# Two graph layers on one core: the neighbours' rows of three tiles in eight are fetched from DRAM by index instead of being selected by one-hot matmuls

## The chip, the cores and the metric

The kernel runs on one core of one Trainium2 chip. The metric is the device time of one execution in microseconds (us); lower is better. Three executions of the kernel before the change took 2499.42, 2499.82 and 2503.61 us, so the median is 2499.82 us.

Names of engines in this document: PE is TensorE (matmuls and transposes; PEld is its weight load), DVE is VectorE, ACT is ScalarE, POOL is GpSimd, SP is the engine that issues the DMAs of the kernel before. "L499" is line 499 of the kernel.

## The reference, cut to what matters

There are 16 graphs ("images" below) of 1024 nodes with 64 features each, and a 1024x1024 matrix of small integers for each graph that tells which nodes are neighbours. Two attention layers follow each other, each with a residual and a normalisation of the rows.

```python
x = -0.0005207 + 1.001 * jax.random.normal(..., (16, 1024, 64), jnp.float32)
_a = jax.random.bernoulli(..., 0.00390625, (16, 1024, 1024))
_a = jnp.logical_or(_a, jnp.swapaxes(_a, -1, -2))
adj = jnp.logical_or(_a, jnp.eye(1024, dtype=bool)).astype(jnp.int32)

def _L0_gnn_ref(atom_embeddings, edges, Wq, bq, Wk, bk, Wv, bv, edge_bias, Wp, bp):
    q = (atom_embeddings @ Wq + bq).reshape(b, m, h, d)      # h = 8 heads, d = 64
    k = (atom_embeddings @ Wk + bk).reshape(b, m, h, d)
    v = (atom_embeddings @ Wv + bv).reshape(b, m, h, d)
    scores = jnp.einsum('bmhd,bnhd->bhmn', q, k) * scale
    scores = scores + jnp.transpose(edge_bias[edges], (0, 3, 1, 2))
    scores = jax.nn.leaky_relu(scores, NEG_SLOPE)
    scores = jnp.where((edges > 0)[:, None, :, :], scores, -1000000000.0)
    attn = jax.nn.softmax(scores, axis=-1)
    out = jnp.einsum('bhmn,bnhd->bmhd', attn, v).reshape(b, m, h * d)
    return out @ Wp + bp

def _L1_gnn_ref(h, adj, lin_w, lin_b, W_w, a):
    hp = jnp.einsum('bni,oi->bno', h, lin_w) + lin_b
    s = u[:, :, None, :] + v[:, None, :, :]                  # u, v: hp times the halves of W_w
    e = jnp.einsum('bijf,f->bij', jnp.where(s > 0, s, ALPHA * s), a[:, 0])
    attention = jax.nn.softmax(jnp.where(adj > 0, e, NEG_INF), axis=2)
    return jax.nn.elu(jnp.einsum('bij,bjf->bif', attention, hp))

x = _layernorm(x + _L0_gnn_ref(x, adj, ...))
x = _layernorm(x + _L1_gnn_ref(x, adj, ...))
```

The matrix has few entries: a node has about eight neighbours among 1024, and itself.

## The kernel before

**Groups and slots.** The kernel does not compute all 1024x1024 scores. It puts the 1024 nodes of an image into 128 groups of 8 consecutive nodes (GR = 8). For each group it lists the columns that any of its 8 nodes needs, in 120 *slots* (SLOTS): 112 for neighbours, which are found from the matrix, and 8 for the group's own nodes. Scores, exponentials and weighted sums are taken over these 120 slots. A mask (`finish`, L423) blanks the slots that belong to another node of the group.

**Tiles and steps.** The 128 groups of an image make 8 *tiles* (t = 0 to 7) of 16 groups: two halves n of the partitions, 8 groups q in each. One loop, L883, runs over g = 8b + t, b being the image. In one step layer 0 works on several tiles at different stages (gather of tile g, turn and score of tile g - 1, exponentials and weights of tile g - 2, output of tile g - 3), and layer 1 does the same for the image before, 12 steps later (LAG). The order of the instructions of every engine is the order in which the loop writes them; no scheduler changes it. Each engine works through its own list in order, so an instruction that waits holds all behind it on the same engine.

**Lists.** `prepare(b)` (L308) builds the lists of an image: DVE turns the matrix into keys and takes the largest of them eight at a time. It is a generator; `Lists.place` (L858) is called at five places of each step and advances it by so many pieces that image b's 41 pieces (PIECES, dealt out by QUOTA) are done two steps before its first tile. After a piece that yields "sums" it goes on only at the step's last place, because the next piece needs a PSUM bank that PE's weighted sums use. The result, `col`, goes to DRAM (`col_d`, L397), one row of column numbers for each group.

**The gather that is changed.** For a tile, SP loads its lists broadcast to all 128 partitions (`load`, L460: 544 KB, tile `cb`); DVE compares them twice with the partition number, which gives the one-hot matrix `f` (`indicate`, L468, L475); PE multiplies the image's rows, split into three bf16 parts (`t3`), with it (`gather`, L488, L499: 26 matmuls for each half of the slots), and ACT copies the result to `xg` (L505), which has features on the partitions and slots in the rows. `own` (L481, L484) has POOL copy the group's own 8 nodes into the last slots. A step later `turn` (L509, L518, L519) transposes `xg` on PE into `xn`, with slots on the partitions, in 8 transposes and two copies on ACT. `score` reads `xg`, `attend` reads `xn`. Layer 0 and layer 1 each do all this for every tile, with buffers of their own.

**What else POOL does, in its order in a step.** The divisions of tile g - 2 (`divide`, L637), one for each half, each waiting for DVE's reciprocal; when lists are built, the blanking of the diagonal (L327); in step t = 2 the normalisation of layer 0's result of the image before (`end`, L697, by L549 to L552), and in steps 6 and 7 layer 1's residual (L820) and normalisation; the own copies of layers 0 and 1 (L484); the row product of layer 1 (`own_rows`, L728); and at the end of steps 2 and 6 the three-part split of the next layer's input (`thirds`, L445, L451 and L453). `place` number 0 is at the start of a step, ahead of the divisions; number 1 after the second division; 2 and 3 before the own copies; 4 after the row product, at the end of the step.

## Time and profile before

One execution was profiled. It took 2508.74 us; its span from the first to the last instruction is 2506.8 us.

| | us | share of the span |
|---|---|---|
| median of three executions | 2499.82 | |
| the profiled execution | 2508.74 | |
| its span | 2506.8 | |
| line 499, the one-hot matmuls on PE | 804.5 | 32% |
| line 475, the equality tests on DVE | 491.6 | 20% |
| line 637, the divisions on POOL | 285.8 | 11% |
| line 518, the transposes of `turn` on PE | 273.9 | 11% |
| line 519, their copies on ACT | 277.3 | 11% |
| line 505, the gather's copies on ACT | 271.5 | 11% |
| line 728, the row products on POOL | 145.9 | 6% |
| line 484, the own copies on POOL | 107.2 | 4% |

The lines count both layers: 256 tiles, of which 128 are layer 0's. Busy time is the time in which an engine has an instruction running; matmuls overlap, so 52 matmuls of 0.28 us each take about 3 us together. PE's granted clock is 0.988 of full speed on average. All DMAs are issued by SP, and together they keep the 16 DMA engines busy for 28.3% of the span; 230.66 MB are moved.

### The profile page before, as it was taken

How to read it: one execution, taken by the hardware profiler on the slowest of the kernel's cores; microseconds unless marked ns; L12 is line 12 of the kernel's file. 1: busy time of each engine (PE TensorE's matmuls, PEld its weight loads, DVE VectorE, ACT ScalarE, POOL GpSimd, SP SyncE). 2: the span in 40 equal slices, each digit the busy share in tenths (PEclk: the TensorE clock that was granted, in tenths of full speed). 3: DMA queues.
4: the chain of work that ended last, by engine and by line, in shares of the span. 5: the costliest groups of instructions: out<-in, count | busy, mean ns of one | idle time of the engine just before them, and what ended most of it. 6: DMA issues, size and time to landing. Idle time of an engine off the chain costs nothing. (4 is left out here: it accounts for less than half of the span.)

```text
span 2506.8 us, 110853 instructions
## 1 busy us (share of the span) xinstructions
PE 2308.1 (92%) x48706; PEld 1957.7 (78%) x48706; DVE 2012.1 (80%) x5237; ACT 1445.2 (58%) x4401; POOL 912.9 (36%) x1106
## 2 busy tenths in 40 slices
PE   5387999999999999999999999999999999999986
PEld 3376788878788887878788787888878888888864
DVE  6687879888888988888898888889888888876642
ACT  0154656656565665656566566656656665666743
POOL 1133333434334343433434343342434434243331
PEclk9998999999999999999999999999999999999998
DMA  3412332423233242323324232332423233221210
GB/s 102 122 59 89 104 103 78 133 77 116 73 102 108 78 133 80 114 73 107 103 78 133 84 109 75 106 103 78 133 86 108 81 100 106 62 92 57 66 52 18
DMA packets 190543, 230.66 MB, mean 92 GB/s; under 512 B 91492, under 2 KB 157092, under 8 KB 190052
## 3 DMA queue, kind: packets, MB, share of 16 engines
q1 hardware_dynamic: 190052, 223.49, 28.3%
q8 instruction: 384, 6.29, 1.0%
q14 instruction: 107, 0.88, 0.1%
HBM read 218.23 MB, written 5.21 MB: 89 GB/s over the span
## 5 line engine op out<-in xcount | busy, mean ns | idle before, releaser
L499 PE MATMUL pg<-f,x 128*64 128x272 bf16 (+2 forms) x13312 | 804.5, 272 | 37.4 <-DVE f L475 34.5
L499 PEld LDWEIGHTS <-x 128*64 128x64 bf16 x13312 | 662.0, 109 | 115.5 <-issue 70.4
L637 POOL TENSOR_TENSOR ls<-ls,den 128x480 f32<-128x480 f32 x256 | 285.8, 1117 | 921.1 <-DVE den L636 912.6
L475 DVE TENSOR_SCALAR f<-cb,jrow 128x2176 bf16<-128x2176 bf16 x512 | 491.6, 1001 | 0.3 <-DMA cb<-col_d 0.3
L505 ACT COPY xg<-pg 128x448 f32<-128x448 f32 x512 | 271.5, 530 | 356.1 <-PE pg L499 355.1
L629 ACT ACTIVATE ls<-ls,mx 128x120 f32<-128x120 f32 x1024 | 391.2, 386 | 4.8 <-DVE mx L620 4.8
L519 ACT COPY xn<-pt 120x512 f32<-120x512 f32 x512 | 277.3, 597 | 11.8 <-PE pt L518 7.1
L751 ACT ACTIVATE r<-pz 128x480 f32<-128x480 f32 x256 | 132.1, 568 | 247.0 <-PE pz L746 247.0
L518 PE MATMUL pt<-ident,xg 128*120 128x128 f32 x2048 | 273.9, 276 | 0.0
L484 POOL COPY xg<-xT 128x64 f32<-128x64 f32 x256 | 107.2, 426 | 387.9 <-PE pt L518 345.4
L518 PEld LDWEIGHTS pt<-ident,xg 128*120 128x120 f32 x2048 | 224.0, 137 | 27.3 <-issue 24.8
L752 DVE SCALAR_TENSOR_TENSOR r<-pz,r 128x480 f32<-128x480 f32 x256 | 155.4, 649 | 50.6 <-ACT r L751 50.6
L629 ACT ACTIVATION_READ_ACCUMULATOR ls<-ls,mx 128x1 f32 x1024 | 194.8, 190 | 0.0
L619 DVE SCALAR_TENSOR_TENSOR ls<-sc 128x480 f32<-128x480 f32 x256 | 191.5, 748 | 0.0
L620 DVE TENSOR_REDUCE mx<-ls 128x4 f32<-128x480 f32 x256 | 167.2, 653 | 8.8
L611 DVE TENSOR_TENSOR sc<-s,rowc 128x480 f32<-128x480 f32 x256 | 155.1, 647 | 22.7 <-PE s L603 21.0
L746 PEld LDWEIGHTS pz<-rw,ub 64*64 64x64 f32 x4096 | 122.6, 133 | 63.9 <-issue 58.5
L655 PE MATMUL z<-w,xn 120*64 120x64 f32 x4096 | 159.2, 227 | 4.4 <-ACT w L647 4.4
L587 DVE TENSOR_TENSOR qp<-pq,qb 128x512 f32<-128x512 f32 x128 | 87.9, 686 | 90.0 <-PE pq L586 89.8
L655 PEld LDWEIGHTS z<-w,xn 120*64 120x64 f32 x4096 | 138.4, 139 | 27.7 <-ACT w L647 19.4
L645 PE MATMUL pp<-ident,ls 128*120 128x128 f32 x1024 | 142.0, 280 | 19.3 <-POOL ls L637 16.6
L740 PE MATMUL pz<-xg,w2d 64*64 64x480 f32 x1024 | 140.4, 588 | 17.1 <-DVE sc L611 17.1
(212 smaller groups left out, 3881.1 us busy)
## 6 DMA issues: line engine op xcount, KB each, us to landing
cb<-col_d SPq DMA_DIRECT2D x256, 544.0 KB
ad<-in_adj_dram SPq DMA_DIRECT2D x256, 256.0 KB
xs<-in_x_dram SPq DMA_DIRECT2D x32, 128.0 KB
rows_s<-slot_d SPq DMA_DIRECT2D x256, 14.0 KB
out_dram<-o SPq DMA_DIRECT2D x32, 128.0 KB
col_d<-col SPq DMA_DIRECT2D x128, 4.2 KB
dg<-in_adj_dram SPq DMA_DIRECT2D x32, 2.0 KB
slot_d<-slot SPq DMA_DIRECT2D x16, 28.0 KB
```

The source lines that it names most:

```text
L475: nc.vector.tensor_scalar(fj.rearrange("p s n q k -> p (s n q k)"), cb.rearrange("p s n q k -> p (s n q k)"), jrow[:, j : j + 1], None, AL ...
L499: nc.tensor.matmul(pg[sub(n), :, FIRST * a_ + lo : FIRST * a_ + to], self.t3[:, k, 4 * hs + 2 * a_ + j, :], f[j][:, 2 * hs + a_, n, :, lo:to],
L505: nc.scalar.copy(dst, pg)
L518: nc.tensor.transpose(pt[:, q, :], xg[:, 4 * m + q, :], ident)
L519: nc.scalar.copy(self.xn[t][:, ts(m, 4), :], pt)
L611: nc.vector.tensor_tensor(sc, both[n], self.rowc[:, n, ts_].unsqueeze(2).to_broadcast([P, 4, SLOTS]), ALU.add)
L619: nc.vector.scalar_tensor_tensor(ls, scs[n], SLOPE, scs[n], ALU.mult, ALU.max)
L620: nc.vector.tensor_reduce(self.mx[:, n, ts_], ls, XX, ALU.max, negate=True)
L629: nc.scalar.activation(ls[:, q, :], ls[:, q, :], AF.Exp, bias=neg[:, q : q + 1], accum_out=den[:, q : q + 1])
L637: nc.gpsimd.tensor_tensor(ls, ls, den.unsqueeze(2).to_broadcast([P, 4, SLOTS]), ALU.mult)
L655: nc.tensor.matmul(zz[sub(n), q, :], xn[:, q, sub(n)], w_[n][:, q // 2, sub(q % 2)], start=True, stop=True)
L752: nc.vector.scalar_tensor_tensor(r, pz[n], SLOPE / (1.0 - SLOPE), r, ALU.mult, ALU.add)
```

## The change

In each image, the tiles T = 2, 5 and 7 of layer 0 no longer get their slots' rows by one-hot matmuls. The five other tiles, and all of layer 1, are unchanged.

A copy of the image's rows is put into a DRAM table with one more row at its front (`table`), in a new place of `start`. `prepare` makes, at its end, a row number for each of the 120 slots of each of the 128 groups, turns it by one PE transpose so that slots lie on the partitions, and keeps it as integers (`at_d`). For a fetched tile POOL issues 16 indirect DMAs, one for each group: each takes 120 row numbers from one column of `at_d` and brings 120 rows of 64 values (256 bytes each) into the group's part of the buffer `xf`, which takes the place of `xn`. The gather of such a tile is then 8 transposes from `xf` into `xg`, and `load`, `indicate`, `own` and `turn` do nothing for it.

```diff
+    FETCHED = {2: (0, 1), 5: (2, 3, 4), 7: (5, 6)}
...
         def place(self, g, k):
+            b, t = divmod(g, NT)
+            for T, steps in FETCHED.items():
+                if b in l0 and t in steps:
+                    i, parts = steps.index(t) * PLACES + k, len(steps) * PLACES
+                    for j in range(2 * NQ * i // parts, 2 * NQ * (i + 1) // parts):
+                        l0[b].fetch(T, j)
             b, t = divmod(g + AHEAD, NT)
...
+        def fetch(self, t, k):
+            if k == 0:
+                self.xn[t] = dbl.tile([SLOTS, NQ, P], F32, tag="xf", bufs=2, name=f"xf_{self.b}_{t}")
+            n, q = divmod(k, NQ)
+            g = D * n + NQ * t + q
+            nc.gpsimd.indirect_dma_start(
+                out=self.xn[t][:, q, sub(n)], out_offset=None, in_=self.table[:, :],
+                in_offset=bass.IndirectOffsetOnAxis(ap=self.at[:, g : g + 1], axis=0),
+            )
...
+        def gather(self, t, hs):
+            if t not in FETCHED:
+                return super().gather(t, hs)
+            nm = f"{self.b}_{t}"
+            if hs == 0:
+                self.xg[t] = dbl.tile([P, NQ, SLOTS], F32, tag="xg0", bufs=2, name=f"xgf_{nm}")
+            pt = ps_g.tile([P, 4, SLOTS], F32, tag="g", name=f"ptf_{nm}_{hs}")
+            for q in range(4):
+                nc.tensor.transpose(pt[:, q, :], self.xn[t][:, 4 * hs + q, :], ident[0:SLOTS, 0:SLOTS])
+            nc.scalar.copy(self.xg[t][:, ts(hs, 4), :], pt)
```

So tile 2 is fetched in steps 0 and 1, tile 5 in steps 2, 3 and 4, tile 7 in steps 5 and 6. The 16 fetches are spread over the places: with two steps, places 0 to 4 of a step issue 1, 2, 1, 2 and 2 fetches; with three, one at each place, and two at the very last. Each half gather needs four groups q of both halves n of the partitions; the last fetches are those that the second half gather needs.

```diff
     def start(b):
...
+        table = dram.tile([N + 1, D], F32, tag="table", bufs=3, name=f"table_{b}")
+        nc.sync.dma_start(table[0:1, :], x[b, 0:1, :])
...
+            nc.sync.dma_start(
+                table[1 : N + 1, :].rearrange("(t n r) d -> n t r d", n=2, r=D)[n],
+                x[b, n * 512 : n * 512 + 512, :].rearrange("(t r) d -> t r d", r=D),
+            )
...
     def prepare(b):
...
+        yield
+        tb = per.tile([P, NSEG, WIN], F32, tag="tb", name=f"tb_{b}")
+        nc.vector.tensor_tensor(tb, seg_at.unsqueeze(2).to_broadcast([P, NSEG, WIN]), win, ALU.subtract)
+        nc.vector.scalar_tensor_tensor(tb, who, 0.5, tb, ALU.is_ge, ALU.mult)
...
+        nc.vector.tensor_copy(av[:, :, 0:FIRST], tv[:, :, 0, 0:FIRST])
+        nc.vector.tensor_tensor(av[:, :, FIRST:WIN], tv[:, :, 0, FIRST:WIN], tv[:, :, 1, 0:SHARE], ALU.max)
+        nc.vector.tensor_copy(av[:, :, WIN:CAP2], tv[:, :, 1, SHARE:WIN])
+        nc.vector.tensor_copy(at_s[:, 2 * CAP2 : SLOTS], own_at)
+        yield "sums"
+        pi = ps_z.tile([SLOTS, P], F32, tag="z", name=f"pi_{b}")
+        nc.tensor.transpose(pi, at_s, ident)
+        at_d = dbl.tile([SLOTS, P], I32, tag="at_d", name=f"at_d_{b}")
+        nc.vector.tensor_scalar(at_d, pi, 0.0, float(N), ALU.max, ALU.min)
```

A few constants for the row numbers (`own_at`, `seg_at`) are made once at the start. Image lists now have 43 pieces instead of 41, and QUOTA gives the two more to its last two steps. Four buffers become fewer: `mask` has 3 instead of 4, and layer 1's `xT`, layer 0's `y` and layer 1's `u` have 1 instead of 2.

## The prediction, made before the changed kernel ran

> **What bounds the kernel now.** I read the engine totals first, then one image's eight steps (b = 7), then that image's event lists. The steps run from one score product of layer 0 (line 603) to the next; in all images but the first they repeat within a few tenths of a us, so one stands for sixteen.
>
> ```profile
> PE 2308.1 (92%) x48706; PEld 1957.7 (78%) x48706; DVE 2012.1 (80%) x5237; ACT 1445.2 (58%) x4401; POOL 912.9 (36%) x1106
> ```
> ```profile
> core 0: us, PE busy (x) PEld busy (x) DVE busy (x) ACT busy (x) POOL busy (x), PEclk, DMA share, GB/s
> 1202.90:1221.33 18.43, 17.82 (x378) 14.99 (x378) 15.13 (x42) 9.55 (x27) 4.58 (x5) 1.00 0.21 68
> 1221.33:1238.72 17.39, 17.39 (x347) 14.39 (x345) 12.22 (x26) 12.58 (x43) 6.32 (x9) 1.00 0.55 185
> 1238.72:1259.16 20.44, 18.75 (x410) 16.03 (x409) 17.97 (x51) 9.77 (x28) 10.38 (x12) 1.00 0.09 31
> 1259.16:1278.26 19.10, 17.25 (x373) 14.96 (x370) 18.64 (x45) 11.83 (x38) 6.05 (x8) 1.00 0.22 68
> 1278.26:1296.70 18.44, 17.44 (x382) 14.88 (x378) 15.91 (x43) 10.62 (x32) 3.77 (x5) 1.00 0.40 127
> 1296.70:1312.26 15.56, 15.56 (x342) 13.69 (x338) 13.27 (x32) 10.87 (x33) 3.84 (x5) 1.00 0.12 41
> 1312.26:1330.18 17.92, 17.92 (x413) 15.63 (x409) 14.54 (x36) 12.02 (x37) 5.30 (x6) 1.00 0.26 69
> 1330.18:1349.36 19.18, 18.66 (x413) 15.50 (x409) 17.25 (x44) 12.95 (x43) 16.60 (x20) 1.00 0.61 202
> ```
>
> The columns are stretch, length, then busy time per engine. In steps 1, 5 and 6 (second, sixth, seventh row) PE is busy for the whole step: a us taken from PE there is a us of the total. In steps 2 and 3 DVE has 17.97 of 20.44 and 18.64 of 19.10, and PE waits on it, so PE time saved there buys less. POOL looks idle, but it holds 16.60 of 19.18 in step 7.
>
> **What is removed.** One fetched tile drops 52 one-hot matmuls (line 499; the 52 of step 5 took 2.98 us) and, a step later, 8 transposes (line 518, 1.04); its new gather does 8 transposes of a similar shape in the old place, 0.55 per half. PE gains 2.98 - 1.10 + 1.04 = 2.9 us a tile. DVE drops two equality tests (line 475, 2 x 1.0) in the step before; ACT trades four copies (2 x 0.53 + 2 x 0.60) for two of 128x480 (about 0.56 each, between those rows); POOL drops one own copy (0.43), SP one load of 544 KB. With all of it on the path, 48 tiles x 2.9 = 140 us.
>
> **What is added and cheap.** Per image: seven DVE operations of at most 128x136, priced by lines 393, 401 and 782 at about 2 x 0.30 + 4 x 0.17 + 0.29 = 1.6 us, in steps 4 and 5, where DVE has over 2 us spare, and against 6 us of tests removed: nothing. One PE transpose, 0.27 (line 780): 16 x 0.27 = 4 us, on the path; it could also wait for DVE's list, but lists are issued places earlier. Three SP issues copying x, 3 x 0.63 (line 290), ahead of the next image's four mask loads; SP spends 340 us waiting for free buffers of those loads, which hides them; without that cover 1.9 us an image. The head, where lists and copies run alone, grows by the 1.6 of DVE and about 3 of SP and landing: 5 us. Buffers cut to one: y waits for a POOL result two steps old, u and xT1 for POOL copies of the same step; before, xT1's copy on ACT ran at 1259.27, 3.5 us after the POOL copy it now waits for, and three fetches stand ahead of that copy. It can be a few tenths late, then delays the exponentials queued on ACT behind it, and ACT is 58% busy. The mask's third buffer is free again a batch earlier: nothing.
>
> **What is added and dear: 48 fetches an image on POOL.** No indirect DMA is in the trace, so two prices are bounded. *c*, POOL's time for one: from below the DMA issues on SP, at 0.57 for the 64-row list (line 397); from above POOL's slowest operation, the power at 1.86 (line 550). Neither is near, so I take the middle, 1.2. *L*, from end of issue to data usable:
>
> ```profile
> 1316.60 0.76 SPq L408 DMA_DIRECT2D slot_d<-slot  x1
> 1320.34 6.14 SPq L415 DMA_DIRECT2D rows_s<-slot_d  x16
> ```
>
> The second is held by the first: 1320.34 - 1317.36 = 3.0 us (mean of 16 waits 48.9/16 = 3.06). At the start, with idle queues, the same pair took 1.16, and the last small row load 1.73 until DVE could use it. L is 1.16 to 3.06; beside running loads the middle of the last two, 2.4.
>
> POOL must issue the last two fetches of a tile after the row product (line 728) of the step before, and PE needs them for its second half gather early in the next step:
>
> ```profile
> 1295.06 1.04 POOL L728 TENSOR_TENSOR ub<-u,in_q 128x512 f32<-128x512 f32 x1
> 1297.89 2.98 PE L499 MATMUL pg<-f,x 128*64 128x272 bf16 x52
> 1300.70 0.28 PE L280 MATMUL back<-lin,aT 128*64 128x64 f32 x4
> ```
> ```profile
> 1321.21 0.99 POOL L637 TENSOR_TENSOR ls<-ls,den 128x480 f32<-128x480 f32 x1 [4.88 <-DVE den L636]
> 1327.18 1.37 POOL L327 TENSOR_TENSOR ab<-ab,no_diag 128x128 bf16<-128x128 bf16 x2 [4.92 <-DVE ab L324]
> 1328.51 1.76 POOL L820 TENSOR_TENSOR y<-y,x 128x512 f32<-128x512 f32 x1
> 1330.21 1.11 POOL L484 COPY xg<-xT 128x64 f32<-128x64 f32 x2
> 1331.29 1.22 POOL L728 TENSOR_TENSOR ub<-u,in_q 128x512 f32<-128x512 f32 x1
> 1332.45 0.60 POOL L451 CAST x<-xs 128x512 bf16<-128x512 f32 x1
> ```
>
> Tile 5 (step 5): row product over at 1296.1, two fetches 2.4, landing 2.4, half gather 0.55: 1301.45. Before, the gather was over at 1300.87. Loss 0.6, less the 1.04 saved in step 6: gain 0.45 us.
>
> Tile 7 (step 7): after the division at 1322.2 come five fetches (6.0), to 1328.2; then what is queued behind them: diagonal mask 1.37, addition 1.76, one own copy 0.5, row product 1.2, to 1333.0; then the last two 2.4, landing 2.4, half gather 0.55: 1338.35 against 1335.07 before (1332.43 + 2.64). Loss 3.3, less 1.04: 2.25. The divisions of step 7 slip too, but PE asks for them later, at some 1342.
>
> Tile 2 (step 2): POOL has slack in steps 0 and 1; counted the same way from the division that ends at 1213.6, the last fetch ends at 1240.8 and lands at 1243.2. PE's second half began at 1244.1, held by DVE's sums (a 1.02 wait of line 671). No stall, but the first half's 0.94 only lengthens that wait; what stays is about 1.0 of the rest, since steps 2 and 3 are DVE's.
>
> Sum per image: 1.0 + 0.45 - 2.25 = -0.8, so +13 us in all; transpose and head +9. DVE is slowed too: a pair of tests beside an idle POOL took 1.47, beside POOL's work 2.24 to 2.74. Steps 2 and 3, DVE's own, hold about six tests each with others; with POOL busy half again as long I take 0.2 more for each of six on the path: 1.2 x 16 = +19. Bounds: none, or 0.5 for each, +48. Altogether 13 + 9 + 19 = +41 on the profiled execution's 2508.74 (span 2506.8): 2550. Its time stands 0.36% above the median, so 2541 there.
>
> The Trainium skill (SBUF — State Buffer, section "SBUF: two separate sides") speaks against the change: while DVE runs a two-port operation, POOL cannot write descriptors, and a DMA of some 620 ns took about 3100. Should that strike both last fetches of tiles 5 and 7 by 2.5 us each, the estimate by that page would be 10 us an image more, some 2700. DMA: Bandwidth & Descriptors (section on the anatomy of one DMA, the gpsimd path) gives about 2.0 us for a whole small DMA; in place of my 3.6 for issue and landing, that estimate would be 3.2 us an image less, about 2490. No run so far shows either.
>
> **Rivals.** *Fetches are short and land early* (c = 0.57, L = 1.16, no DVE slowing): tile 5 has no stall and gains 2.9; tile 7's last pair follows the unchanged 1332.5, is usable at 1335.35 after the half gather, -0.3 + 1.04 = 0.8; tile 2 gives 1.0. 4.7 x 16 = 75 less, 9 back: 2443, or 2434 by the median. With c = 1.0 and L = 1.73: 1.0 + 1.5 - 0.6 = 1.9 an image, 31 less, 9 back, so 2478 by the median. For it: POOL is 36% busy. Against: the place of the last pair, which no small c moves before 1332.5. It ends faster while c stays below about 1.1 and DVE is not slowed. *POOL becomes the bound*: POOL has 57 us of work in an image of 146, and 48c fit while c < 1.85; but steps 0, 1, 5 and 6 take eight each. At c = 1.5, L = 2.5 the same counts give tile 2 -0.5, tile 5 -0.3, tile 7 -4.5: 5.3 x 16 = 85, with 9: 2594 by the median; at 1.86 and 3.06 the sum is about -16 an image, 2764. *The gain and the stalls cancel*: c near 1.15 and no DVE slowing, 2500. That the change does not do what it says is excluded: the issue order shows 48 fetches an image on POOL, and the one-hot products gone.
>
> **How the numbers follow.** Moderate stalls with DVE slowed, the forecast, 2510 to 2570: 0.35. POOL bound, above 2570: 0.20. Short fetches: 0.36. Cancelling: 0.09. A measurement of this kernel tells about 0.2% from no change, so: faster 0.36, same 0.09, slower 0.55. The likeliest case alone spans 2510 to 2570; the range reaches to c of about 0.6 on one side and 1.7 on the other: 2430 to 2640.
>
> **What would show it.** Each second-half transpose of a fetched tile has PE idle before it, waiting for a DMA: 2 to 6 us in step 7, 1 to 3 in step 5, none in step 2. POOL's fetch group has a mean near 1.2 us and POOL's busy time rises from 913 to some 1,800 (913 - 20 + 768 x 1.2). Line 475's mean goes above 1.0 us. Wrong if PE's waits for fetches sum under 30 us, or if POOL is idle when PE waits.

## The result, and the profile after

Four executions of the changed kernel took 2646.8 to 2661.52 us, median 2658.88, beside 2501.72 us for the kernel before: a ratio of 1.0616, 95% interval 1.0579 to 1.0653. It is slower by 6.2%. The forecast was 2541 us; the measured time lies above the top of its range, 2640. The profiled execution's span is 2657.7 us against 2506.8.

The page of the changed kernel: engine totals, the DMA queue of the new fetches, the group of the fetches, and the equality tests.

```profile
PE 2273.4 (86%) x46226; PEld 1890.6 (71%) x46226; DVE 1950.1 (73%) x5261; ACT 1395.9 (53%) x4305; POOL 1681.1 (63%) x1829
...
q0 software_dynamic: 24576, 23.67, 4.9%
...
L611 POOL DMA_INDIRECT xf<-table,at_d x768 | 826.5, 1076 | 202.4 <-issue 187.3
...
L514 DVE TENSOR_SCALAR f<-cb,jrow 128x2176 bf16<-128x2176 bf16 x416 | 360.2, 907 | 0.3 <-DMA cb<-col_d 0.3
```

The priced parts of the fetch came out as forecast: 1.08 us for one, and with the gap before it (202.4/768 = 0.26) 1.34 us; POOL went from 913 to 1681 us. The equality tests (line 475 before, 514 now) did not get slower: 907 ns against 1001. PE lost only 35 us of busy time, where 140 had been counted: part of what is left runs slower, because PE's clock falls, as shown below.

The image b = 7 by steps, with the columns of the table of before; steps 2, 7 and 0 of the next image:

```profile
1161.34:1181.64 20.30, 16.95 (x367) 14.22 (x366) 18.41 (x57) 9.96 (x28) 14.15 (x13) 1.00 0.15 44
...
1254.74:1279.37 24.63, 19.29 (x369) 14.97 (x366) 15.07 (x41) 12.89 (x43) 20.04 (x25) 0.86 0.50 158
1279.37:1296.88 17.51, 16.47 (x370) 14.03 (x369) 15.07 (x43) 8.48 (x25) 9.25 (x10) 1.00 0.18 41
```

Step 7 stands out: PE is busy for 19.29 of 24.63 us, at a granted clock of 0.86, and POOL for 20.04. Over images 2 to 13 the median lengths of the steps, before and after, are:

| step | 1 | 2 | 3 | 4 | 5 | 6 | 7 | 0 |
|---|---|---|---|---|---|---|---|---|
| before, us | 17.66 | 20.40 | 19.09 | 18.44 | 15.56 | 17.93 | 18.77 | 17.58 |
| after, us | 18.31 | 20.88 | 17.80 | 20.09 | 17.06 | 17.45 | 25.11 | 17.52 |

Step 7 alone is 6.34 us longer; the other seven add 2.5 us together. The granted clock changed with them: in these twelve images it fell to half of full speed not once before, and 33 times after, for 157 us together: 12 times in step 7, and 21 times in steps 2 to 5. Step 4, for instance, takes 20.9 us in the six images in which it falls there, and 18.6 to 19.3 in the six others. What PE waited for in the changed kernel (total us, times, longest):

```profile
PE ptf L636 <- DMA xf<-table,at_d: 121.0, 73, 3.9
PE e L845 <- DVE r L831: 50.1, 65, 2.1
PE po L750 <- DVE sc L690: 46.5, 29, 2.1
PE pi L456 <- DVE at_s L453: 38.5, 15, 23.4
```

The first is the new wait for fetched rows. The second and third were 17.7 and 27.7 us before: where PE has less to do, it comes to DVE's results earlier and waits there. The fourth is the new transpose of the row numbers, 23.4 us of it at the head.

PE's instructions at the start of step 7 (start, duration, idle time before and its releaser in brackets). Line 682 is the score product, 636 the new transposes of the gather, 665 and 819 the first two products behind it:

```profile
1254.74 1.05 PE L682 MATMUL s<-xg,qp 64*64 64x120 f32 x32
...
1255.93 0.73 PE L636 MATMUL ptf<-ident,xf 120*128 120x120 f32 x5
1259.49 0.32 PE L636 MATMUL ptf<-ident,xf 120*128 120x120 f32 x1 [2.83 <-DMA xf<-table,at_d]
1262.32 0.72 PE L636 MATMUL ptf<-ident,xf 120*128 120x120 f32 x2 [2.51 <-DMA xf<-table,at_d]
...
1263.24 1.92 PE L665 MATMUL pq<-xT,aqk 128*64 128x64 f32 x32
1265.09 1.88 PE L819 MATMUL pz<-xg,w2d 64*64 64x480 f32 x8
```

Two waits, 5.34 us together, and behind them two groups that took 1.10 and 1.03 us in the steps of before take 1.92 and 1.88. Line 665 starts 8.5 us after the score product here (8.5 to 9.8 in images 1 to 13), against 4.12 in most images before: 4.8 us later at a mean of 8.9. With 0.82 and 0.85 for the two groups that makes 6.5, which is about the whole growth of the step.

POOL's list at the same time, from the third-last fetch of tile 7 on:

```profile
1252.82 1.96 POOL L611 DMA_INDIRECT xf<-table,at_d  x1 [0.30 <-issue]
1254.79 0.82 POOL L349 TENSOR_TENSOR ab<-ab,no_diag 128x128 bf16<-128x128 bf16 x2
1255.57 1.27 POOL L899 TENSOR_TENSOR y<-y,x 128x512 f32<-128x512 f32 x1
...
1256.98 1.03 POOL L807 TENSOR_TENSOR ub<-u,in_q 128x512 f32<-128x512 f32 x1
1258.20 1.03 POOL L611 DMA_INDIRECT xf<-table,at_d  x1 [0.19 <-issue]
1259.53 1.35 POOL L611 DMA_INDIRECT xf<-table,at_d  x1 [0.30 <-issue]
```

The third-last fetch is over at 1254.78, used at 1259.49, so 4.7 us to land, while SP issued four mask loads and two list loads between 1251 and 1256.5. The last two follow the row product (807). The second-last is over at 1259.23 and used at 1262.32, 3.1 us later; the last is over at 1260.88 and landed some 1.7 us later, in time for the last transpose. PE's clock over these microseconds (the number after POOL's count), then the DMA share, which falls as the loads end:

```profile
1259.00:1260.00 1.00, 0.32 (x1) 0.14 (x1) 1.00 (x3) 0.00 (x0) 0.69 (x2) 1.00 1.10 402
1260.00:1261.00 1.00, 0.00 (x0) 0.00 (x0) 0.97 (x3) 0.00 (x0) 0.99 (x2) 0.63 0.97 393
1261.00:1262.00 1.00, 0.00 (x0) 0.00 (x0) 0.96 (x2) 0.00 (x0) 0.91 (x2) 0.50 0.36 121
1264.00:1265.00 1.00, 1.00 (x22) 0.97 (x20) 0.00 (x0) 0.40 (x3) 0.98 (x1) 0.50 0.00 0
1267.00:1268.00 1.00, 1.00 (x36) 0.84 (x30) 0.00 (x0) 0.03 (x1) 0.54 (x1) 0.95 0.00 0
```

The clock is halved 3.6 us after PE fell idle at 1256.66, with one transpose in between, and is back at 1267.1, after 6.8 us. The Trainium skill (TensorE: Matmul & The Clock Gate, section "Part 1: The HAM clock gate (the "warmup" mystery)") says that an idle window of about 3.4 us halves the clock and as long a busy stretch restores it. The rows agree in kind, and the 33 stretches at half speed last 3.41 us or two or three times that; but shorter gaps were enough too, as tile 2 and the filler show below, and there the measurement decides.

### The profile page after: what moved, and what is told of

Read it like the earlier page. It is cut to its first block, busy times and chain, and to the rows that moved or that the text cites. A ratio compares the mean times of both kernels' runs of the same rounds, so it can differ in the third digit from the quotient of the medians.

```text
span 2657.7 us, 106517 instructions
## 1 busy us (share of the span) xinstructions
PE 2273.4 (86%) x46226; PEld 1890.6 (71%) x46226; DVE 1950.1 (73%) x5261; ACT 1395.9 (53%) x4305; POOL 1681.1 (63%) x1829
## 3 DMA queue, kind: packets, MB, share of 16 engines
q1 hardware_dynamic: 184164, 200.95, 24.6%
## 5 line engine op out<-in xcount | busy, mean ns | idle before, releaser
L611 POOL DMA_INDIRECT xf<-table,at_d x768 | 826.5, 1076 | 202.4 <-issue 187.3
L538 PE MATMUL pg<-f,x 128*64 128x272 bf16 (+2 forms) x10816 | 671.3, 276 | 11.7 <-DVE f L514 11.1
L538 PEld LDWEIGHTS <-x 128*64 128x64 bf16 x10816 | 546.3, 111 | 83.3 <-issue 43.5
L544 ACT COPY xg<-pg 128x448 f32<-128x448 f32 x416 | 220.4, 530 | 267.2 <-PE pg L538 263.1
L514 DVE TENSOR_SCALAR f<-cb,jrow 128x2176 bf16<-128x2176 bf16 x416 | 360.2, 907 | 0.3 <-DMA cb<-col_d 0.3
L558 ACT COPY xn<-pt 120x512 f32<-120x512 f32 x416 | 225.5, 597 | 14.2 <-PE pt L557 11.0
L557 PE MATMUL pt<-ident,xg 128*120 128x128 f32 x1664 | 223.5, 277 | 0.0
L636 PE MATMUL ptf<-ident,xf 120*128 120x120 f32 x384 | 78.1, 312 | 121.1 <-DMA xf<-table,at_d 121.0
L665 PE MATMUL pq<-xT,aqk 128*64 128x64 f32 x4096 | 164.7, 242 | 0.1
L724 PE MATMUL pp<-ident,ls 128*120 128x128 f32 x1024 | 142.6, 281 | 19.1 <-POOL ls L716 17.9
L665 PEld LDWEIGHTS pq<-xT,aqk 128*64 128x64 f32 x4096 | 153.2, 157 | 1.6 <-issue 0.6
```

Source lines behind the costliest of these rows:

```text
L514: nc.vector.tensor_scalar(fj.rearrange("p s n q k -> p (s n q k)"), cb.rearrange("p s n q k -> p (s n q k)"), jrow[:, j : j + 1], None, AL ...
L538: nc.tensor.matmul(pg[sub(n), :, FIRST * a_ + lo : FIRST * a_ + to], self.t3[:, k, 4 * hs + 2 * a_ + j, :], f[j][:, 2 * hs + a_, n, :, lo:to],
L544: nc.scalar.copy(dst, pg)
L557: nc.tensor.transpose(pt[:, q, :], xg[:, 4 * m + q, :], ident)
L558: nc.scalar.copy(self.xn[t][:, ts(m, 4), :], pt)
L611: nc.gpsimd.indirect_dma_start(out=self.xn[t][:, q, sub(n)], out_offset=None, in_=self.table[:, :], in_offset=bass.IndirectOffsetOnAxis(ap ...
```

## The experiments

Runs listed together ran on one chip, beside runs of the kernel before there; the ratio is to those. After the first four, the question was how the loss divides among the tiles; after the next eight, what was wrong with tile 7, and what the lists cost.

### The parts, taken away: lists only, no fetches, fetches unused, earlier fetches

*Lists only.* Nothing is fetched; the table, the row numbers and the smaller buffers stay.

```diff
-    FETCHED = {2: (0, 1), 5: (2, 3, 4), 7: (5, 6)}
+    FETCHED = {}
```

> No tile is fetched: the table, the row numbers, the 43 pieces and the smaller buffers stay, all tiles gather by one-hot matmuls. Theory A (the loss is PE waiting for rows that land late, and its clock falling after each wait): 2505 to 2525 us, the +9 of the prediction. Theory C (lists and smaller buffers cost): more than 2580.

Measured: 2528.28 us, ratio 1.0099 (1.0069 to 1.0128), 3 us above theory A's range. At 2504.21 us for the kernel before beside it, the lists cost 24 us.

*No fetches.* The transposes read a constant tile, so the rows of the three tiles are constants.

```diff
-                self.xn[t] = dbl.tile([SLOTS, NQ, P], F32, tag="xf", ...)
+                self.xn[t] = const_xf
...
-            nc.gpsimd.indirect_dma_start(...)
```

> The indirect DMAs are left out; the three tiles are transposed from a constant tile, so the output is not the reference's. All of the PE, DVE and ACT work saved is saved, nothing can be late. Theory A: 2400 to 2450 (2.9 us a tile less, some of it lost in steps 2 to 4 where DVE sets the pace), granted clock back above 0.97. Theory C: above 2550.

Measured: 2493.25 us, ratio 0.9956 (0.9936 to 0.9975); neither theory's range holds it. Its engine totals and two waits of PE:

```profile
PE 2202.6 (89%) x46226; PEld 1850.8 (74%) x46226; DVE 1965.1 (79%) x5262; ACT 1389.9 (56%) x4305; POOL 904.0 (36%) x1061
```
```profile
PE e L842 <- DVE r L828: 46.1, 68, 1.9
PE po L747 <- DVE sc L687: 38.9, 28, 2.0
```

Against the lists alone, PE has 111 us less to do (2313.7 to 2202.6) and the time falls by 35. The two waits for DVE are 41.6 us there and 85.0 here. So even fetches that cost nothing at all would bring this change 0.4%. In step 2 the saved work even turns into a loss. PE's wait for DVE's sums grows from 1.0 to 2.0 us, and in seven of the images 2 to 13 the clock falls behind it: those steps take 20.9 to 21.2 us, the five others 19.7, and with the lists alone 20.4.

*Fetches unused*, the one-hot gather kept for all tiles; and all tiles' fetches *one place earlier*, of which this is the edit:

```diff
-                    i, parts = steps.index(t) * PLACES + k, len(steps) * PLACES
+                    i, parts = steps.index(t) * PLACES + k, len(steps) * PLACES - 1
...
```

> All 768 fetches are issued into their buffers, but nobody reads them: the three tiles are gathered by one-hot matmuls as before. Theory A: 2510 to 2540, little above the lists alone, since POOL has room and nothing waits for the data. Theory B (the fetches slow DVE by the shared port, or hold up POOL's divisions and row products): above 2600.

> Each tile's 16 fetches end one place earlier, ahead of the own copies and the row product, at the same number a step. Theory A: the last pair is issued some 2 to 3 us earlier against PE, PE's wait for rows falls from 121 to below 60 us, the time to 2560 to 2610. Theory B or C: within 20 us of the changed kernel's 2659.

Measured: 3049.37 us (ratio 1.218) and 3079.38 us (1.230, interval 1.2237 to 1.2363). The first lies in its theory B's range, the second in none, but neither theory's cause is what the traces show. In both, ACT and DVE stood waiting for PE's semaphores long after PE had passed the instruction; the wait list of the second calls the releaser "remote", a word that the changed kernel's own list does not have:

```profile
ACT xg L544 <- remote: 220.2, 51, 17.1
DVE eT L861 <- remote: 209.9, 48, 6.5
```

These waits lay beside runs of four to six fetches issued back to back, which made that issue a suspect. The suspicion is taken up below; it fell.

### One tile at a time, and PE kept busy in the gap

```diff
-    FETCHED = {2: (0, 1), 5: (2, 3, 4), 7: (5, 6)}
+    FETCHED = {2: (0, 1)}          # and {5: (2, 3, 4)}, and {7: (5, 6)}
```

> The table, the slot numbers and the smaller pools stay; tile 2 alone is fetched (256 indirect DMAs), tiles 5 and 7 are built by the one-hot matmuls again. Theory A (each fetched tile has its own price, set by how long TensorE then waits for its last pieces): the changed kernel's steps around tile 2 are longer than those with the lists alone by about 1.0 us an image, so 2528 + 16 = about 2545 us, and TensorE waits for xf under 15 us in all. Theory B (the price is one of the sheer number of fetches, from 768 on): under 2535. Theory C (the saving on TensorE shows): 2528 - 47 = about 2480.

> Tile 5 alone is fetched, spread over three steps. Theory A: in the changed kernel steps 3 to 5 together are 0.6 us an image longer than with the lists alone, so 2528 + 10 = about 2538 us, TensorE waiting for xf about 15 to 25 us. Theory B: under 2535. Theory C: about 2480.

> Tile 7 alone is fetched. Theory A: steps 6 and 7 of the changed kernel are 5.9 us an image longer than with the lists alone, and image 0 some 10 us, so 2528 + 94 + 10 = about 2630 us, with TensorE waiting for xf about 80 to 100 us: nearly the whole loss is this tile's. Theory B (a third of the fetches, so a third of the loss or less): under 2570.

| | us | ratio (interval) | over the lists alone (1.0099) | PE's wait for rows |
|---|---|---|---|---|
| tile 2 alone | 2549.95 | 1.0198 (1.0169 to 1.0228) | +0.0099 = 25 us | 5.8 us |
| tile 5 alone | 2531.74 | 1.0125 (1.0096 to 1.0155) | +0.0026 = 6.5 us | 26.5 us |
| tile 7 alone | 2627.21 | 1.0507 (1.0477 to 1.0538) | +0.0408 = 102 us | 89.4 us |

All three are within 7 us of what theory A expected (tile 5's time lies in theory B's range as well), and they add: 25 + 25 + 6.5 + 102 = 158 us, against 154 for the whole change (0.0616 x 2501). Two thirds of the loss is tile 7.

Tile 2 costs 25 us though PE hardly waits for its rows. In images 2 to 13, steps 1, 2 and 3 are on average 0.7, 0.7 and 0.3 us longer than with the lists alone. PE's list in step 2 of one image, with the lists alone and then with tile 2 fetched, and the clock there at the end of the wait and behind it:

```profile
1103.85 1.59 PE L538 MATMUL pg<-f,x 128*64 128x272 bf16 x26
1106.45 1.66 PE L750 MATMUL po<-zT,wvp 64*64 64x128 f32 x32 [1.01 <-DVE sc L690]
```
```profile
1115.14 0.63 PE L636 MATMUL ptf<-ident,xf 120*128 120x120 f32 x4
1117.88 2.10 PE L750 MATMUL po<-zT,wvp 64*64 64x128 f32 x32 [2.11 <-DVE sc L690]
1119.91 1.06 PE L636 MATMUL ptf<-ident,xf 120*128 120x120 f32 x4
```
```profile
1117.00:1118.00 1.00, 0.12 (x1) 0.12 (x2) 1.00 (x4) 0.00 (x0) 0.00 (x0) 1.00 0.15 27
1120.00:1121.00 1.00, 1.00 (x6) 0.69 (x8) 0.96 (x2) 0.62 (x2) 0.00 (x0) 0.50 0.02 8
```

DVE's sums come only 0.15 us later; PE comes to them 0.95 us earlier, so its wait grows to 2.1 us. In nine of the twelve images the clock then falls to half, and the step takes 21.1 to 22.6 us. In the three others it stays, and the step takes 20.2 us, less than the 20.4 with the lists alone. So, as the two groups of images in this one run show it, the loss of step 2 is the clock's. The loss of steps 1 and 3 goes with slower operations of DVE. One of them, with the lists alone and with tile 2:

```profile
L389 DVE SCALAR_TENSOR_TENSOR kb<-left,c 128x32 f32<-128x32 int32 x48 | 15.6, 325 | 1.6
```
```profile
L389 DVE SCALAR_TENSOR_TENSOR kb<-left,c 128x32 f32<-128x32 int32 x48 | 25.7, 536 | 1.6
```

This and line 346 of the list building take DVE 25 us more. But it is not the fetches that slow them: in the changed kernel line 346 takes 0.425 us on average where nothing but a fetch runs on POOL beside it (125 times) and 0.422 where POOL is idle, but 0.77 beside one of POOL's element-wise operations (TENSOR_TENSOR in the rows, 86 times). The fetches shift these operations of POOL against DVE's, so that others run side by side than before; that this is the whole of the slowing is not shown.

*Filler.* 18 matmuls whose result is overwritten stand ahead of tile 7's second half, in the changed kernel with all three tiles.

```diff
+            for _ in range(18 if hs and t == 7 else 0):
+                nc.tensor.matmul(pt[:, 0, :], self.xn[t][:, 0, :], ident[0:SLOTS, 0:SLOTS], start=True, stop=True)
             for q in range(4):
                 nc.tensor.transpose(pt[:, q, :], ...)
...
```

> The changed kernel with all three tiles fetched, and 18 idle-time matmuls (the first one's 0.27 us each, 4.9 us together) put on TensorE ahead of tile 7's second half of transposes, where it waits 5.3 us; their result is overwritten, nothing is left out. Theory A (the gap also lowers the granted clock, and matmuls right behind it run at half speed for some 4 us): the two groups behind the gap go back from 1.92 and 1.88 us to about 1.1 and 1.05, the mean clock from 0.946 to 0.96 or more, and the time falls by 1.5 to 2 us an image, to 2625 to 2635 us. Rival (the clock falls for another reason): the two groups stay at 1.9 us, and the time stays at 2655 to 2670.

Measured: 2641.83 us, ratio 1.0566 (1.0535 to 1.0596). That is less than theory A expected. In the image looked at, the fillers ended 1.6 us too early (an idle time of 1.64 us before the last two transposes), and the clock fell all the same: 0.92, 0.50, 0.50, 0.50, 0.87 in the five microseconds behind. With 26 fillers:

> The changed kernel with 26 instead of 18 filler matmuls ahead of tile 7's second half (about 6.1 us at 4.18 us for the 36 multiplied passes of 18). With 18, TensorE still stood idle for 1.64 us and the granted clock was at 0.5 for 3.2 us behind it. Theory A (any gap of that size costs the clock): with the gap closed, the two groups behind it run in 1.10 and 1.04 us, TensorE's waits for xf fall from 64 to under 35 us, the clock rises from 0.960 to 0.97 or more, and the time falls by another 20 to 28 us, to 2612 to 2625. Rival (the remaining loss of step 7 is not the clock's): 2635 to 2650.

Measured: 2631.21 us, ratio 1.0508 (1.0477 to 1.0538), below the changed kernel's interval. The end of the gap:

```profile
1252.53 0.50 PE L638 MATMUL ptf<-ident,xf 120*128 120x120 f32 x2 [0.46 <-DMA xf<-table,at_d]
...
1253.12 1.10 PE L667 MATMUL pq<-xT,aqk 128*64 128x64 f32 x32
1254.15 1.04 PE L821 MATMUL pz<-xg,w2d 64*64 64x480 f32 x8
```

The two groups are back at 1.10 and 1.04 us. Line 665 starts as late as in the changed kernel (9.0 us after the score product on average, 8.9 there), so nothing but the speed behind the gap differs: the clock is worth about 27 us in step 7 (0.0616 - 0.0508 = 0.0108; by the intervals 15 to 39), 1.7 an image, as the two groups' 0.82 and 0.85 say. The time itself lies between the two theories' ranges: less remains to be had from the clock than A put there.

### Tile 7's place, spaced fetches, and the row numbers

Tile 7 alone, its 16 fetches dealt over nine places instead of ten, so that none follows the row product; all tiles one place earlier with a memset of 128x256 on POOL behind each fetch; and, with nothing fetched, one more piece boundary between the row numbers and their transpose (`yield` ahead of `yield "sums"`, 44 pieces; QUOTA, which deals the pieces out to the steps, goes from (3, 3, 5, 6, 6, 6, 7, 7) to (3, 3, 5, 6, 6, 7, 7, 7)).

```diff
-                    i, parts = steps.index(t) * PLACES + k, len(steps) * PLACES
+                    i, parts = steps.index(t) * PLACES + k, len(steps) * PLACES - 1      # tile 7 alone
...
```
```diff
+            nc.gpsimd.memset(spare, 0.0)                                                 # behind each fetch
```

> Tile 7 alone is fetched, as in the run that took 2627, but its 16 fetches are dealt over nine places instead of ten, so that the last pair is issued before GpSimd's own copy and row product instead of behind them. Theory A (the loss is the last pair's place in GpSimd's queue): TensorE's waits for xf fall from 89 to under 20 us, and the time to 2530 to 2550. Theory B (a denser run of fetches brings the waits for semaphores that the run with all three tiles one place earlier showed, 3079 us): steps 5 and 6 grow by 5 us or more each, waits put down to remote appear, and the time is above 2650.

Measured: 2580.94 and 2604.43 us, ratio 1.0354 (1.0242 to 1.0466): neither. No remote waits, but PE still waits 42.3 us for rows. SP, POOL and PE around one start of step 7:

```profile
1210.26 1.28 SPq L322 DMA_DIRECT2D ad<-in_adj_dram  x2
1210.78 1.40 POOL L611 DMA_INDIRECT xf<-table,at_d  x1 [0.30 <-issue]
1212.49 1.08 POOL L611 DMA_INDIRECT xf<-table,at_d  x1 [0.31 <-PE pa L870]
1213.08 1.31 SPq L322 DMA_DIRECT2D ad<-in_adj_dram  x2
1218.19 0.46 PE L636 MATMUL ptf<-ident,xf 120*128 120x120 f32 x1 [2.84 <-DMA xf<-table,at_d]
1219.36 0.46 PE L636 MATMUL ptf<-ident,xf 120*128 120x120 f32 x1 [0.70 <-DMA xf<-table,at_d]
```

The last two fetches are issued by 1213.57, before PE needs them, and used at 1218.19 and 1219.36, 6.0 and 5.8 us after the end of their issue, beside four loads of the next image's mask and two list loads of 544 KB. Moving them off POOL's late work put them onto the loads.

> All three tiles one place earlier, as in the run that took 3079 us, with a GpSimd memset of 128x256 behind each fetch, so that no two fetches follow each other without work between them. Theory B1 (it is the back-to-back issue of fetches that holds up other engines' semaphores): the remote waits fall to under a quarter of that run's 620 us, and the time to below 2750. Theory B2 (it is the fetches' number or traffic, or the earlier places as such): the remote waits stay, 3000 us or more.

Measured: 2668.42 us, ratio 1.0657 (1.0626 to 1.0688), no remote waits: what theory B1 expected. The next runs take its support away.

> Lists only, nothing fetched, as in the run that took 2528; one more piece boundary between the last vector operation on the row numbers and their transpose, so that TensorE comes to the transpose a place later. Theory A (of the 24 us that the lists cost, the transpose's wait for the vector engine is 15 to 18): 2508 to 2516, and the wait before that transpose under 0.3 us in all images but the first. Rival (the 24 us come from the smaller pools or the copies in DRAM): 2522 to 2532.

Measured: 2531.91 us, ratio 1.0111 (1.0082 to 1.0141). PE's wait before the transpose fell from 37.0 to 24.6 us, all but 1.2 of it at the head, and the time did not move. The steps say why: step 5 fell from 16.67 to 15.82 us at the median, but step 3 rose from 19.10 to 19.76, because the new QUOTA puts one more piece of DVE's list building there, where DVE was already busy for 18.63 us. The run moved the cost, and doesn't decide between its two theories.

### Clear of the loads; the same kernel on another chip; the lists' parts

```diff
-                    i, parts = steps.index(t) * PLACES + k, len(steps) * PLACES
+                    i, parts = steps.index(t) * PLACES + k, len(steps) * PLACES - 3      # tile 7 alone
...
```

> Tile 7 alone is fetched, its 16 fetches dealt over seven places instead of ten, so that the last is issued some 5 us before SP issues step 7's mask loads and list load (in the run with nine places the last pair was issued beside them and took 6.0 and 5.8 us to land). Theory A (the landing is long because those loads hold the DMA engines): no wait of TensorE for xf above 1 us, under 15 us in all, step 7 at 17.5 to 18.5 us, and 2530 to 2550 us, near the 2528 of the lists alone. Rival (a fetch lands late whatever runs beside it, or denser fetches slow the other engines): above 2565.

Measured: 2515.98 us, ratio 1.0059 (1.0039 to 1.0079). PE waits for rows once, for 1.0 us; step 7 takes 18.75 us at the median. In image 7 the last fetch is over at 1186.57 and SP's loads of step 7 begin at 1187.64. Tile 7 now gains 10 us on the lists alone (1.0099 - 1.0059), where it had cost 102, and the time beats theory A's range. Yet the steps in which its work is saved are no shorter: steps 7 and 0 take 18.75 and 17.52 us, 18.77 and 17.58 with the lists alone, though PE is busy for 1.4 and 1.0 us less in them. The gain is in step 5, 15.91 us against 16.67, and comes from the row numbers, as shown below.

> All three tiles with their fetches one place earlier, once more, on another chip than the one on which it took 3079 us with 620 us of remote waits. If those waits belong to the kernel (fetches issued back to back), 3000 to 3100 again. If they belong to that chip, the landing times seen since give 2590 to 2650, near the spaced run's 2668, and no remote waits.

Measured: 2552.37 us, ratio 1.0205 (1.0184 to 1.0225), no remote waits, with the kernel that had taken 3079.38. One place earlier is thus worth some 106 us to the changed kernel. That is below both ranges that had been set. The long waits of the first time don't come with back-to-back fetches alone, but with something on the first chip, and the spaced run's 2668 is no cure: it is 116 us slower than the same kernel without the memsets. The run with unused fetches was made on that first chip only, and its 3049 us says nothing here.

The pools alone (the kernel before with the four smaller buffers) and the lists without the three copies of x into the table, which nothing reads there:

```diff
-        mask = dbl.tile([P, NT, SLOTS], BF16, tag="mask", bufs=4, name=f"mask_{b}")
+        mask = dbl.tile([P, NT, SLOTS], BF16, tag="mask", bufs=3, name=f"mask_{b}")      # xT, y, u likewise
```
```diff
-        nc.sync.dma_start(table[0:1, :], x[b, 0:1, :])
...
```

> The kernel before with only the four smaller pools (mask 3 for 4, layer 1's xT, layer 0's y and layer 1's u 1 for 2). Theory A (the 24 us of the lists come from the pools): 2512 to 2525. Theory B (they come from the row numbers and the copies): 2498 to 2506.

> Lists only, without the three DMAs an image that copy x into the table; nothing reads the table, so nothing is missing. Theory A (the copies delay the next image's loads behind them on SP): 2508 to 2518. Theory B (they are hidden, as predicted): 2523 to 2532.

Measured: 2503.18 us, ratio 1.0005 (0.9996 to 1.0015), and 2527.24 us, ratio 1.0101 (1.0084 to 1.0118). Neither the pools nor the copies cost anything. What is left are the row numbers, and the trace shows how they cost. The end of step 5 with the lists alone, and the same operation in the run with tile 7 over seven places:

```profile
1175.36 1.09 POOL L807 TENSOR_TENSOR ub<-u,in_q 128x512 f32<-128x512 f32 x1
1175.58 1.02 DVE L446 SCALAR_TENSOR_TENSOR tb<-who,tb 128x136 f32<-128x136 int32 x1
1177.23 0.30 PE L456 MATMUL pi<-ident,at_s 128*120 128x128 f32 x1 [0.81 <-DVE at_s L453]
```
```profile
1170.03 1.50 POOL L611 DMA_INDIRECT xf<-table,at_d  x1 [0.30 <-issue]
1171.62 0.30 DVE L446 SCALAR_TENSOR_TENSOR tb<-who,tb 128x136 f32<-128x136 int32 x1
```

Line 446 takes 1.02 us in 13 of the 16 images with the lists alone, beside POOL's row product, and 0.30, the price given to it, in the first three. In the run with tile 7 over seven places and in the one with the later transpose it runs beside fetches or nothing and takes 0.30 in all 16. PE stands behind it: 0.81 us of waiting and 0.30 for the transpose, which is the 1.1 us by which step 5 is longer. Over all images the waits outside the head are 13.6 us and the transposes 4.8: 18 of the 24 us. This is read from the traces; a kernel without the row numbers alone was not run.

### All early, and without tile 2

```diff
+    LEAD = {2: 1, 5: 1, 7: 3}
-                    i, parts = steps.index(t) * PLACES + k, len(steps) * PLACES
+                    i, parts = steps.index(t) * PLACES + k, len(steps) * PLACES - LEAD[T]
```
```diff
-    FETCHED = {2: (0, 1), 5: (2, 3, 4), 7: (5, 6)}
+    FETCHED = {5: (2, 3, 4), 7: (5, 6)}            # with LEAD = {5: 1, 7: 3}
```

> All three tiles fetched; tiles 2 and 5 end one place earlier, tile 7 three places earlier, clear of step 7's loads. In the last run with one place for all, step 7 alone was still long (22.90 us against 18.77). Theory A (that step's wait is all that is left): 2552 less 16 x 4.1 = about 2487 us, faster than before by 0.4 to 0.8%, TensorE's waits for xf under 15 us, the clock at 0.98 or more. Rival (denser fetches on GpSimd slow the vector engine and the divisions): 2505 to 2530.

> Tiles 5 and 7 alone, ending one and three places earlier. Theory A (tile 2 is the one that gains nothing: its steps 2 and 3 belong to the vector engine, and fetched alone it cost 22 us over the lists): faster than the run with all three by 10 us or more, 2470 to 2485. Rival (tile 2 pays once its fetches are early): slower than it.

Measured over five rounds: 2505.37 us, ratio 1.0017 (1.0005 to 1.0030), and 2477.34 us, ratio 0.9901 (0.9884 to 0.9918). In the first the waits for rows are gone (5.9 us), so placing takes back nearly all of the 154 us. But theory A's 2487 was too low, and so was the clock, 0.972 for the 0.98 or more that it expected: in step 2 it falls in seven of the images 2 to 13 (20.5 to 23.5 us; 19.1 to 20.3 in the others). The rival's range holds the time, just, but this part of the loss is not the one it named. In the second, tile 2 left out brings 28 us, as expected, and in images 2 to 13 the clock doesn't fall once. It is faster than both kernels, by 1.0% against the one before. Its totals and its wait for rows:

```profile
PE 2229.6 (90%) x47058; PEld 1880.3 (76%) x47058; DVE 1965.3 (80%) x5293; ACT 1406.7 (57%) x4337; POOL 1446.8 (59%) x1589
```
```profile
PE ptf L636 <- DMA xf<-table,at_d: 4.5, 4, 2.2
```

## Why the prediction was wrong

Its side was right, its size was not: +41 us was forecast on the profiled execution, +151 came. By its own terms:

| term | predicted, us | measured, us | by |
|---|---|---|---|
| tile 7 | 2.25 x 16 = 36 | 102 | tile 7 alone over the lists |
| tile 2, with DVE's slowing | -16 + 19 = 3 | 25 | tile 2 alone |
| lists: transpose and head | 9 | 25 | lists only, and without copies |
| tile 5 | -0.45 x 16 = -7 | 6.5 | tile 5 alone |

**The fetch's price held.** c was taken as 1.2 and measured 1.08 (1.34 with the gap before it). POOL was expected at some 1,800 us, and was 1681.

**The step that failed is "Loss 3.3, less 1.04: 2.25" for tile 7.** Its mechanism stands: the last pair waits behind the diagonal mask, the addition, the own copy and the row product. In image 7 of the changed kernel the end of the second half gather is nearly where it was put: 1338.35 - 1330.18 = 8.17 us after the score product, measured 1263.04 - 1254.74 = 8.30. Some of that is luck: the pair was over 0.9 us later than reckoned, and its last landing was 0.7 us shorter than the 2.4; and image 7 is the earliest of images 1 to 13. Three things were wrong around it. The loss is 4.8 us, not 3.3: the image taken as the pattern of before was a late one (by the loop's count it is b = 8), where line 586 started 4.80 us after its score product, against 4.12 in most, which makes 0.7 of the difference; half of the rest is that line 665 starts at 8.93 on average after the change, and at 8.50 in image 7. The clock was put at nothing, although the page prints it: a PE that stands idle for some 5 us then works for some 5 us at half speed, 1.7 us an image, and the run with 26 fillers shows it. And the 1.04 us credited for the transposes saved in step 0 did not come: 17.58 before, 17.52 after.

**"L is 1.16 to 3.06" was too narrow on one side.** By the semaphores in the trace, the 768 fetches of the changed kernel took 1.4 to 7.4 us to land, median 1.9. Where the other DMA queues were busy for under 5% of the time it was 1.7 (378 fetches), where they were busy for over half of it 3.7 (155 fetches). So the 2.4 was high for most and too low for what stands beside SP's mask and list loads: 4.7 for tile 7's third-last fetch, and 6.0 and 5.8 with nine places. The prediction's table shows a DMA share of 0.61 in step 7, which is those loads, but L was priced from small loads of another step. The 2.0 us for a whole small DMA, from which it had an estimate of 2490, was too little: from the start of the issue to the landing the median was 3.0.

**"A us taken from PE there is a us of the total" failed.** With no fetch at all, 111 us less PE work brought 35. With tile 7 fetched in time, PE had 1.4 and 1.0 us less to do in steps 7 and 0, and neither was shorter. So PE, it seems, was busy nearly throughout because its work just filled the time that DVE's and ACT's results took: without the fetches its waits for DVE's results grew by 43 us. The prediction's own rows showed DVE at 80% of the span.

**Tile 2, "no stall": a clock that wasn't priced.** "The first half's 0.94 only lengthens that wait" was right, and counted as harmless. A wait of 2.1 us in place of 1.0 let the clock fall in nine of twelve images, and those steps are some 1.3 us longer than the three others.

**For the lists the step that failed is "it could also wait for DVE's list, but lists are issued places earlier".** It waited in every image, 13.6 us outside the head, because an operation priced at 0.30 took 1.02 beside POOL's row product. The transposes themselves took 4.8 us, for the 4 in the sum. The pools and copies that were priced at nothing cost nothing.

**DVE's slowing came in another place and from another cause.** 1.2 us an image were put on line 475 for a POOL that is busy half again as long. But the mean of the tests fell to 907 ns: beside a fetch alone they took 782 (221 times), beside nothing 778, beside POOL's element-wise operations 1179 (131 times; 209 times and 1303 before). What grew were operations of the list building that now run beside such operations of POOL: line 346 has a mean of 541 ns (445 before), line 389 of 720 (280), together 45 us more. The Trainium skill (SBUF — State Buffer, section "SBUF: two separate sides") led to expect fetches held up to five times their length; of 768 the longest took 1.96 us and the median 1.02. That its estimate of some 2700 us lies near the result is luck.

**Rivals.** "Short fetches" is out for the change as placed: the second-half gather of tile 7 ends where the place of the last pair puts it, as the objection to this rival said, although c, at 1.08, was under the 1.1 that it asked for. With the place changed, fetches of the same c pay, 2477 us without tile 2. "POOL becomes the bound" gave 2594 to 2764, and the time lies in there, but not by its mechanism: POOL is busy for 63% of the span, c is below the 1.5 that it needed, and 102 of 158 us are one tile's last pieces.

## What to carry to other kernels

A transfer that another engine waits for is priced by what runs on the DMA engines between its issue and its use, and by what stands ahead of it in the issuing engine's list; look at both for the very last piece, because it alone sets the end, and move it clear of both. An engine that is busy throughout is not for that the bound: take its work away in thought and ask which engine's result it would then wait for. And an idle gap on PE costs twice, once as a wait and once as slow matmuls behind it; work taken from PE in front of such a wait makes the gap longer and can lose more than it saves. When one engine gets new work, look at which of its old operations are pushed beside another engine's.

## What the runs showed of the hardware

- An indirect DMA of 120 rows of 256 bytes held POOL for 0.98 to 1.96 us, median 1.02, with 0.30 us between two in a row. From the end of its issue to its landing it took 1.4 to 7.4 us in the changed kernel: median 1.7 with the other queues busy for under 5% of the time, 3.7 with them busy for over half of it.
- Two or three waits of 5.2 to 6.6 us together in step 7 of the changed kernel brought the clock to half in all images 2 to 13, for 6.8 us, once 10.2. Behind a single wait of 2.1 us (tile 2 alone) it fell in nine of twelve images, behind one of 1.0 us at the same place in none. In the run with 18 fillers it fell in one image after 1.64 us, for 3.4.
- DVE's equality tests on 128x2176 took 0.78 us beside a fetch alone as beside an idle POOL, and 1.18 on average beside POOL's element-wise operations; an operation on 128x136 with int32 input took 0.30 us beside a fetch and 1.02 beside POOL's row product.
- One kernel took 3079 us on one chip and 2552 on another, while the kernel before it took 2504 and 2502 on the two. On the first, ACT and DVE waited for PE's semaphores for mostly 3 to 6.5 us at a time while POOL issued fetches in a row; the kernel without fetches and the one with lists only were undisturbed there. What differs between the chips was not tried, and the cause stays open.
